# Moving small constant loads, value weights, the seam into attention, the gates and the operand sums of keys and values in a two-batch decoder kernel

## The chip, the core and the metric

The kernel is one program on one core of one Trainium2 chip. Its time is what the device needs for one execution, in microseconds (us). The engines of a core run side by side and wait for one another through semaphores: TensorE (PE in the profile) for matmuls, VectorE (DVE), ScalarE (ACT) and GpSimd (POOL) for elementwise work, and SyncE (SP), which here only issues transfers. All arithmetic is in float32 but for the quantized product, whose operands are whole numbers in bfloat16.

## The reference

Two batches of 512 tokens with 1024 features each, and a context of 1024 tokens for each batch, go through four residual steps. `ln` is a layer norm without weights.

```python
x = x + fake_quant(ln(x)) @ fake_quant(ctx)              # 8-bit grid, one scale and zero point a side
h = ln(x)                                                # 8 low-rank experts of rank 16, mixed
q = h[:, 179:-1, :].mean(1)                              # by a softmax over the mean token
r = softmax(q @ router_W.T + router_b)
x = x + h @ W.T + b + 2 * sum_e(r_e * (h @ A_e.T) @ B_e.T)
h = ln(x)                                                # 32 query heads, 8 key and value heads
Q, K = rope(h @ wq), rope(ctx @ wk); V = ctx @ wv
x = x + softmax(Q @ K.T / sqrt(128) + mask) @ V @ wo
h = ln(x)                                                # 4 experts of rank 8, the best one a token
x = x + h @ W_up.T + (h @ A_e.T) @ B_e.T, e = argmax(h @ gate_w.T + bias)
```

## The kernel before

**Products by seven.** Every large product is cut into two by two blocks and made with seven block products instead of eight, from sums of blocks. `left_steps` makes four sums for one side (`s1`, `s2`, a new `a21`, `s4`), `right_steps` four for the other (`t1`, `t2`, a new `b12`, `t4`), one instruction each. `seven` runs the block products in the order 1, 2, 6, 7, 5, 4, 3. Products 1 and 2 use blocks as they were loaded; product 6 wants `s2` and `t2`, product 7 the new `a21` and `b12`, product 3 `s4`, product 4 `t4`. Products 1 and 2 share one bank of PSUM (the accumulators beside TensorE), 7 and 4 another, 5 and 3 a third; VectorE reads a bank before the next product adds to it (L288 to L300). A block product of keys, queries or values is 4 or 8 matmuls and takes TensorE 3.43 us; a float32 matmul leaves two records in the profile.

**Stages.** In order: keys and values of batch 0 (`keys`, `values`, heads in two halves `q`), with the quantized product of batch 0 and then of batch 1 laced in (`layer_0` through `weave`); keys and values of batch 1, then with the layer norm and router of batch 0 (`routed`) laced in; the second step's products (`linear`); queries of both batches (`queries`), the last of them inside the beginning of attention; attention over 64 heads of queries with the output projection laced in; the last linear step, whose gates (`gated`) are laced into the end of attention.

**What sets the order.** TensorE's order is that of the program text throughout (`manual_schedule`). In the first product stage VectorE and ScalarE are written out by hand as well, and in attention VectorE, ScalarE and GpSimd. Elsewhere a planner orders each engine's queue, by the order of the text and by when it thinks that data and buffers are there. Each queue, SP's transfers included, runs strictly in the order that it was given. Buffers come from pools by size: 14 of 8 KB a partition (`u8`), 17 of 4 KB (`u4`), 10 of 2 KB (`u2`).

**The places of the change.** Eight small constants (four quantization parameters, two biases, the router's matrix `r0_t`, the gates' matrix `ga_t`) are loaded through POOL's queue at the start (L119 to L146). The first blocks of key weights and context are loaded in four chunks over SP's and ScalarE's queues, and `seven` starts with head group 0 (`m` is the head group in a pair). Value weights are loaded by `quad_weights` (L370) after the key products that stand before them, and summed by VectorE (L245 to L253). `routed` adds the bias on GpSimd (L612) and makes the router's logits with eight matmuls of 8 columns (L630). `queries` rotates heads (L216 to L223) on VectorE, for the last quarter of heads on GpSimd and one step later. In `attention` each head goes through three phases: scores with the mask added (L768, L782); the maximum's tree (L790 to L796) with projections or remaining query products between; then the maximum placed in PSUM (L810), subtracted (L814), the exponential (L817), its sums on GpSimd (L820 to L825) and the product with the values (L831). Maximum and denominator are turned by transposes (L732), written to DRAM as a row and read back to all partitions (L741, L747). At the start of attention `mid` is a head without an `old` one in front of it. `hooks` hangs the work of the last step on heads and phases; `gated` has five stretches: clear, two of matmuls, transposes with the choice of the expert, and the last transposes.

Of the kernel before, what the change touches and what calls it, by code (L numbers as in the profile page):

```python
# [12 lines left out]
F32 = mybir.dt.float32  # L13
BF16 = mybir.dt.bfloat16
AF = mybir.ActivationFunctionType
ALU = mybir.AluOpType
# [23 lines left out]
def decoder_kernel(  # L40
# [66 lines left out]
    make_identity(nc, ident)  # L107
    eps_t = const.tile([P, 1], F32, name="eps_t")
    nc.gpsimd.memset(eps_t, EPS)
    prefer = const.tile([P, E1], F32, name="prefer")  # L110
    for e in range(E1):
# [4 lines left out]
    qp = {}  # L116
    for name, ap in qparams.items():
        t = const.tile([P, 1], F32, name=f"qp_{name}")
        nc.gpsimd.dma_start(t, ap.partition_broadcast(P))  # L119
        qp[name] = t  # L120
    for side in ("x1", "x2"):
        t = const.tile([P, 1], F32, name=f"qp_inv_{side}")
        nc.vector.reciprocal(t, qp[f"{side}_scale"])
        qp[f"{side}_inv"] = t

    c_x1 = const.tile([P, 1], F32, name="c_x1")
    c_x2 = const.tile([P, 1], F32, name="c_x2")
    for c_t, side in ((c_x1, "x1"), (c_x2, "x2")):
        nc.vector.tensor_scalar(c_t, qp[f"{side}_zp"], -1.0, QMID, ALU.mult, ALU.add)
    kc2 = const.tile([P, 1], F32, name="kc2")  # L130
    nc.vector.tensor_scalar_mul(kc2, c_x2, float(D))
    s12 = const.tile([P, 1], F32, name="s12")
    nc.vector.tensor_tensor(s12, qp["x1_scale"], qp["x2_scale"], ALU.mult)
    ident_b = const.tile([P, P], BF16, name="ident_b")
# [3 lines left out]
    rb_t = const.tile([P, E0], F32, name="rb_t")  # L138
    nc.gpsimd.dma_start(rb_t, rb0.partition_broadcast(P))
    eb_t = const.tile([P, E1], F32, name="eb_t")  # L140
    nc.gpsimd.dma_start(eb_t, ebias.partition_broadcast(P))
    r0_t = const.tile([P, NC, E0], F32, name="r0_t")
    nc.gpsimd.dma_start(r0_t, r0T.rearrange("(c p) e -> p c e", p=P))
    NGA = E1 + E1 * R1
    ga_t = const.tile([P, NC, NGA], F32, name="ga_t")
    nc.gpsimd.dma_start(ga_t, gaT.rearrange("(c p) e -> p c e", p=P))  # L146
    cos_t = [const.tile([P, HALF], F32, name="cos_t"), None]
# [121 lines left out]

    def seven(product, emit):  # L270

        banks = {}
        for i in (1, 2, 6, 7, 5, 4, 3):
            first = {2: 1, 4: 7, 3: 5}.get(i, i)
            if i == first:
                banks[i] = ps_b()
            acc = banks[first]  # L280
            product(i, acc, i == first)
            if i == 1:
                u, c22, c21 = u2([P, HALF]), None, None
                nc.scalar.copy(u, acc)
            elif i == 2:
                emit(0, 0, acc)
            elif i == 6:
                nc.vector.tensor_tensor(u, u, acc, ALU.add)  # L288
            elif i == 7:
                c22 = u2([P, HALF])  # L290
                nc.vector.tensor_tensor(c22, u, acc, ALU.add)
            elif i == 5:
                nc.vector.tensor_tensor(c22, c22, acc, ALU.add)  # L293
                emit(1, 1, c22)
            elif i == 4:
                c21 = u2([P, HALF])
                nc.vector.tensor_tensor(c21, u, acc, ALU.add)
                emit(1, 0, c21)
            else:
                nc.vector.tensor_tensor(u, u, acc, ALU.add)  # L300
                emit(0, 1, u)
            yield
# [60 lines left out]

    def quad_weights(dram, q):

        raw = []
        for mh in range(2):
            for ch in range(2):
                w = u4([P, 4, 256])
                nc.sync.dma_start(w, dram[q, mh, ch])  # L370
                raw.append(w)
        return quad_sums(raw)

    def quad_sums(raw):
        return left_sums(nc.vector, *raw, lambda: u4([P, 4, 256]))

# [36 lines left out]
    def context_sums(quarters):  # L413
        return right_sums(nc.vector, *quarters, lambda: u8([P, 4, HALF]))

# [65 lines left out]

    def keys(b, q, ctx_ops, w):
        def group(m):
# [11 lines left out]

            return seven(product, emit)

# [111 lines left out]
    def routed(b, quarters, a_t, b_t, result):  # L609
# [14 lines left out]
        nc.vector.tensor_tensor(qm[:, 0, :], qm[:, 0, :], qm[:, 1, :], ALU.add)  # L624
        nc.vector.tensor_scalar_mul(qm[:, 0, :], qm[:, 0, :], 1.0 / (Q_END - Q_START))
        yield
        yield
        racc = ps_b()
        for c in range(NC):
            nc.tensor.matmul(  # L630
                racc[:, :E0],
                qm[:, 0, c : c + 1].to_broadcast([P, P]),
                r0_t[:, c, :],
                start=(c == 0),
                stop=(c == NC - 1),
            )
        lg = small([P, E0])
# [29 lines left out]

    def queries(q, h_ops, w, later=None):

        def head(m):  # L670
# [7 lines left out]
            def finish(i, j, src):  # L678
                dst = u2([P, HALF]) if (i, j) == (0, 0) else src
                eng = nc.vector if later is None else nc.gpsimd  # L680
                yield from rope_steps(dst, src, 0, ATT_SCALE, eng)
                nc.sync.dma_start(q_d[j][4 * q + 2 * i + m], dst)
# [173 lines left out]
    def attention(extra):  # L856
# [28 lines left out]
        for n in range(-2, total + GRP + 1):  # L885
# [33 lines left out]
            if n > GRP and gg + 1 < B * NKV:  # L919
                for i in {2: (1, 6, 2), 3: (7, 5, 4, 3)}.get(k, ()):  # L920
                    w_ops[i] = output_operand((gg + 1) % NKV, i)
            for _ in range(extra.pop(n, 0)):
                for _ in range(2):
                    next(tree, None)
                next(extra["products"])
            if n == GRP:
                w_ops = {i: output_operand(0, i) for i in (1, 6, 2, 7, 5, 4, 3)}
# [3 lines left out]

            if mid:
                mid.place_maximum()
# [5 lines left out]
            if old:  # L939
                old.attend(0)  # L940
            if mid:
                mid.exponential(0)
            if old:
                old.den = from_row(old.den)
                if new:
                    new.turn_maximum()
            if mid:
                mid.exponential(1)
            if new:
# [92 lines left out]

    for c in range(4):
        cs = slice(c, c + 1)
        nc.sync.dma_start(wk_raw[0][0][:, cs, :], wk[0, 0, 0][:, cs, :])
        load_context(nc.scalar, 0, 0, cs)
# [14 lines left out]
    for ch in range(2):  # L1061
        load_weight(1, 1, ch)


    ctx_ops = [ctx_raw[0], ctx_raw[2]] + [None] * 5
    w = [wk_raw[q][0:2] + [None] * 5 for q in range(2)]
    first = [keys(0, q, ctx_ops, w[q]) for q in range(2)]

# [7 lines left out]
    with tc.manual_schedule(engines={mybir.EngineType.DVE, mybir.EngineType.Activation}):  # L1076
        rights = right_steps(nc.vector, *ctx_raw, lambda: u8([P, 4, HALF]))
        lefts = left_steps(nc.vector, *wk_raw[0], lambda: u4([P, 4, 256]))
        advance(rights, 2)
        advance(lefts, 2)  # L1080
        for g in first[0]:
            next(g)
# [15 lines left out]
        load_rows(0, nc.scalar)  # L1098

    side = layer_0()  # L1100
    for b in range(B):
        if b == 1:
            for ch in range(2):
                ctx_raw[2 * ch + 1] = context_quarter(1, ch, 1, nc.scalar)
            w = quad_weights(wk, 0)
            ctx_ops = context_sums(ctx_raw)
        for i, stage in enumerate((keys, keys, values, values)):
# [6 lines left out]
            if (b, i) == (0, 1):  # L1114
                main = chain(*first[1])
            else:
                main = pair(*stage(b, i % 2, ctx_ops, w))
            weave(main, side, 2)
            if i < 3:
                w = quad_weights((wk, wv)[(i + 1) // 2], (i + 1) % 2)  # L1120
            if i == 1 and b == 1:
# [42 lines left out]
    h_ops = [hb[0][0], hb[0][1]] + [None] * 5  # L1164
    early = [head for q in range(2) for head in queries(q, h_ops, w[q])]
    for _ in range(2):
# [8 lines left out]
    for q in range(NH // 4):  # L1175
        heads = (
            early[2 * q : 2 * q + 2]
            if q < 2
            else queries(q, h_ops, w, later if q == NH // 4 - 1 else None)
        )  # L1180
        main = chain(*heads) if q < 2 else pair(*heads)
        for g in ((0,), (1,), (2,), (3,), (4,), (5,), (6, 7), ())[q]:
            output_sums(g)
        if q < NH // 4 - 1:
            for _ in main:
                pass
            if q > 0:
                w = quad_weights(wq, q + 1)

    extra = {-2: 3, -1: 3, 0: 2, 1: 2, 2: 2, 3: 1, 4: 1}
    steps = attention({**extra, "products": main, "later": later})
# [39 lines left out]
    for i in range(2):  # L1233
# [10 lines left out]
    ]  # L1244
    hooks[(62, 1)] = [lambda: advance(last["gates"], 3)]
    hooks[(62, 2)] = [
        lambda: fetch_weight(7, 0, 1),
        lambda: fetch_weight(3, 1, 1),
    ]
    with tc.manual_schedule(  # L1250
# [6 lines left out]
        for i in range(3 * (B * NH + 2)):  # L1257
# [4 lines left out]
            if (n - 2, phase) == (63, 1):  # L1262
                zT = next(last["gates"])
                h_ops, parts = last["h"], last["w"]
# [4 lines left out]
                main = linear(0, h_ops, w_ops, None, None)  # L1269
                advance(main, 2)  # L1270

    h_ops[:] = token_sums(last["hs"], lambda: u4([P, 4, 256]))
# [122 lines left out]
```

## Time and profile before

| | us |
|---|---|
| median of 3 runs | 2451.58 (2450.20 to 2452.53) |
| the profiled execution | 2450.07 |
| its span in the profile | 2448.30 |
| TensorE busy | 2412.5 (99%) |
| VectorE busy | 1841.1 (75%) |
| GpSimd busy | 1031.3 (42%) |
| ScalarE busy | 530.8 (22%) |

The profile is one execution, seen by the hardware profiler; a line names the engine, the line of the kernel (L355), the operation, the tile written and those read. A wait is put down to what ended last before it. Idle time of an engine counts only where it makes TensorE wait. Before 480 us GpSimd does eight additions in all, beside the issue of transfers and the setting of constants.

### The profile page before, as it was taken

What the parts mean: (1) busy time and instruction counts of PE and PEld (TensorE: products, weight loads), DVE (VectorE), ACT (ScalarE), POOL (GpSimd) and SP (SyncE); (2) the same over time, 40 slices, a digit from 0 to 9 for tenths busy, and PEclk for the clock granted to TensorE, in tenths of its full rate; (3) what the DMA queues carried; (4) which work ended last, traced back from release to release, by engine and by line L of the source; (5) the groups of instructions that cost most, each with busy time, mean ns of one, the idle gap of its engine ahead of it and who ended that gap; (6) DMA issues with size and microseconds to landing.
All of it is one profiled execution on the core that took longest, in us unless ns stands there. A gap on an engine that the chain in (4) does not pass through costs nothing.

```text
span 2448.3 us, 19583 instructions
## 1 busy us (share of the span) xinstructions
PE 2412.5 (99%) x6792; PEld 1195.8 (49%) x6800; DVE 1841.1 (75%) x1994; ACT 530.8 (22%) x623; POOL 1031.3 (42%) x550
## 2 busy tenths in 40 slices
PE   8999999999999999999999999999999999999999
PEld 3477458654444443444444444444444444444444
DVE  4949774345876556898888888888898998888653
ACT  1210221011222222322222222222222222222210
POOL 0000010210000001677676767667776767677621
PEclk9999999999999999999999999999999999999999
DMA  5537133013796221244323323442433343233501
GB/s 182 181 105 273 69 134 108 26 60 116 274 330 216 78 91 56 77 156 111 81 83 107 114 65 90 142 145 79 125 116 79 94 125 112 66 90 108 172 9 60
DMA packets 149010, 288.01 MB, mean 118 GB/s; under 512 B 29424, under 2 KB 47360, under 8 KB 146608
## 3 DMA queue, kind: packets, MB, share of 16 engines
q1 hardware_dynamic: 108080, 244.35, 29.9%
q10 hardware_dynamic: 40400, 41.70, 6.9%
q8 instruction: 54, 0.88, 0.2%
q0 software_dynamic: 432, 0.71, 0.1%
q14 instruction: 44, 0.36, 0.1%
HBM read 223.54 MB, written 63.18 MB: 117 GB/s over the span
## 4 chain that ended last, share of the span: by engine, by line
PE 60%; DVE 6%; POOL 2%; issue 1%; DMA 1%; ACT 1%; ACTq 0%; SPq 0%; DVEq 0%; POOLq 0%
PE b L355 26%; PE wide L768 16%; PE b L831 15%; PE wide L732 2%; DVE u L814 2%; DMA u<-in_wo_dram 1%; DVE u L782 1%; POOL u L823 0%; POOL u L824 0%; DVE small L734 0%; DVE u L792 0%; DVE u L794 0%; ACT u L817 0%; POOL u L825 0%; DVE u L328 0%
## 5 line engine op out<-in xcount | busy, mean ns | idle before, releaser
L355 PE MATMUL b<-u,u 128*128 128x512 f32 (+1 forms) x3616 | 1394.2, 542 | 21.3 <-DMA u<-in_ctxT_in_dram 7.6
L355 PEld LDWEIGHTS b<-u,u 128*128 128x128 f32 x3616 | 684.6, 191 | 695.9 <-issue 612.8
L768 PE MATMUL wide<-u,u 128*128 128x512 f32 x1024 | 454.8, 595 | 7.3 <-DVE u L782 6.4
L831 PE MATMUL b<-u,u 128*128 128x512 f32 x1024 | 460.3, 592 | 0.0
L782 DVE TENSOR_TENSOR u<-wide,u 128x1024 f32<-128x1024 f32 x256 | 312.8, 1224 | 130.3 <-PE wide L768 129.9
L817 ACT ACTIVATE u<-u 128x2048 f32<-128x2048 f32 x128 | 244.7, 1912 | 655.8 <-DVE u L814 593.9
L768 PEld LDWEIGHTS wide<-u,u 128*128 128x128 f32 x1024 | 193.4, 190 | 257.3 <-issue 177.9
L814 DVE TENSOR_TENSOR u<-u,b 128x2048 f32<-128x2048 f32 x128 | 290.2, 2268 | 0.0
L820 POOL TENSOR_TENSOR u<-u 128x1024 f32<-128x1024 f32 x64 | 151.5, 2367 | 317.5 <-ACT u L817 310.1
L831 PEld LDWEIGHTS b<-u,u 128*128 128x128 f32 x1024 | 186.2, 192 | 184.6 <-issue 184.6
L310 POOL TENSOR_TENSOR u<-u,u 128x512 f32<-128x512 f32 x120 | 188.5, 1597 | 175.4 <-DVE u L322 153.2
L328 DVE TENSOR_TENSOR u<-u,b 128x512 f32<-128x512 f32 x200 | 135.8, 680 | 126.0 <-PE b L355 125.9
L222 POOL TENSOR_TENSOR u<-u,sin_t 128x512 f32<-128x512 f32 x8 | 11.6, 1456 | 402.7 <-ACT u L217 402.7
L823 POOL TENSOR_TENSOR u<-u,u 128x1024 f32<-128x1024 f32 x64 | 150.7, 2354 | 36.4 <-ACT u L817 36.0
L824 POOL TENSOR_TENSOR u<-u,u 128x1024 f32<-128x1024 f32 x64 | 150.8, 2356 | 5.0
L842 POOL TENSOR_TENSOR u<-u,u 128x512 f32<-128x512 f32 x64 | 119.9, 1873 | 10.0 <-DMA u<-row 10.0
L216 ACT ACTIVATE u<-u 64x512 f32<-64x512 f32 x72 | 45.2, 628 | 356.3 <-DVE u L293 177.6
L790 DVE TENSOR_TENSOR u<-u 128x1024 f32<-128x1024 f32 x64 | 115.8, 1810 | 0.0
L732 PEld LDWEIGHTS wide<-ident,u 128*128 128x128 f32 x512 | 79.6, 203 | 63.9 <-issue 55.0
L612 POOL TENSOR_TENSOR u<-u,u 128x1024 f32<-128x1024 f32 x8 | 20.2, 2529 | 214.9 <-DVE u L168 111.6
L792 DVE TENSOR_TENSOR u<-u,u 128x1024 f32<-128x1024 f32 x64 | 105.4, 1646 | 0.2
L825 POOL TENSOR_TENSOR u<-u 128x512 f32<-128x512 f32 x64 | 101.0, 1578 | 5.0
(135 smaller groups left out, 1614.3 us busy)
## 6 DMA issues: line engine op xcount, KB each, us to landing
u<-row ACTq DMA_DIRECT2D x128, 256.0 KB, 3.7
u<-wo SPq DMA_DIRECT2D x64, 512.0 KB, 4.0
u<-in_wo_dram SPq DMA_DIRECT2D x48, 512.0 KB, 4.5
u<-in_wq_dram SPq DMA_DIRECT2D x32, 512.0 KB, 4.2
q<-u SPq DMA_DIRECT2D x64, 256.0 KB, 2.4
u<-in_wo_dram SPq DMA_DIRECT2D x16, 1024.0 KB, 8.2
wo<-u SPq DMA_DIRECT2D x32, 512.0 KB, 4.2
u<-q SPq DMA_DIRECT2D x64, 256.0 KB, 4.2
```

The lines of the kernel that those rows point to most:

```text
L310: nc.gpsimd.tensor_tensor(c, c, what, ALU.add)
L328: nc.vector.tensor_tensor(c, c, acc, ALU.add)
L355: nc.tensor.matmul(acc, lhsT, rhs, start=start and k == 0, stop=k == len(pairs) - 1, skip_group_check=True,)
L732: nc.tensor.transpose(tr[:, t, :], src[:, t, :], ident)
L768: nc.tensor.matmul(sc[:, ts(n, HALF)], self.kT[:, ts(2 * j + n, P)], self.qT, start=True, stop=True,)
L782: nc.vector.tensor_tensor(self.e[j // 2][:, js, :], sc.rearrange("p (k q) -> p k q", k=2), mask[j], ALU.add)
L814: nc.vector.tensor_tensor(e, e, self.nmf.unsqueeze(1).to_broadcast([P, 4, S]), ALU.add)
L817: nc.scalar.activation(e, e, AF.Exp)
L820: nc.gpsimd.tensor_tensor(d, e[:, 0:2, :], e[:, 2:4, :], ALU.add)
L823: nc.gpsimd.tensor_tensor(d, d, e[:, 0:2, :], ALU.add)
L824: nc.gpsimd.tensor_tensor(d, d, e[:, 2:4, :], ALU.add)
L831: nc.tensor.matmul(self.acc, self.v[:, k, :], self.e[j][:, k % 4, :], start=(k == 0), stop=(k == NKT - 1),)
```

## The change

It makes six edits. (1) The eight constant loads go from POOL's queue to SP's, behind the loads of the first stage; the first blocks come in three chunks instead of four, the last of double size; both head groups multiply each chunk as it lands (`begun`); and 20 matmuls of `ones_b` by itself are put in front of them, into a bank that the first product overwrites. (2) The raw value weights of batch 0 are taken and loaded before the key products of the second half instead of after them. (3) GpSimd makes the operand sums of keys and values: the six sets of weight sums behind the first two, and the context's sums of batch 1. (4) The router multiplies and adds over its eight chunks on VectorE, so that one matmul by ones is left of eight. (5) At the seam between queries and attention, the last rotation of the last quarter but one waits for attention's third phase; one query product moves from the first head to the second, and that head's exponentials go between the query products. In all heads the denominator's row is read after the second exponential. (6) The gates' transposes and choice come after the third phase of head 62, and their last transposes after two products of the last step.

```diff
-    for name, ap in qparams.items():
-        t = const.tile([P, 1], F32, name=f"qp_{name}")
-        nc.gpsimd.dma_start(t, ap.partition_broadcast(P))
...
-    nc.gpsimd.dma_start(r0_t, r0T.rearrange("(c p) e -> p c e", p=P))
...
-    def seven(product, emit):
+    def seven(product, emit, begun=None):
...
-                banks[i] = ps_b()
+                banks[i] = begun if begun is not None and i == 1 else ps_b()
             acc = banks[first]
-            product(i, acc, i == first)
+            if begun is None or i > 1:
+                product(i, acc, i == first)
...
-    def quad_weights(dram, q):
+    def quad_weights(dram, q, eng=nc.vector):
+        return quad_sums(raw_weights(dram, q), eng)
...
-        return right_sums(nc.vector, *quarters, lambda: u8([P, 4, HALF]))
+        return right_sums(nc.gpsimd, *quarters, lambda: u8([P, 4, HALF]))
...
+        nc.vector.tensor_tensor(
+            weighted,
+            r0_t.rearrange("p c e -> p e c"),
+            qm[:, 0, :].unsqueeze(1).to_broadcast([P, E0, NC]),
+            ALU.mult,
+        )
+        nc.vector.tensor_reduce(each, weighted, AX.X, ALU.add)
         yield
         yield
         racc = ps_b()
-        for c in range(NC):
-            nc.tensor.matmul(
-                racc[:, :E0],
-                qm[:, 0, c : c + 1].to_broadcast([P, P]),
-                r0_t[:, c, :],
...
+        nc.tensor.matmul(
+            racc[:, :E0], one_t.to_broadcast([P, P]), each, start=True, stop=True
+        )
...
-            for _ in range(extra.pop(n, 0)):
+            for i in range(extra.pop(n, 0)):
                 for _ in range(2):
                     next(tree, None)
                 next(extra["products"])
+                if mid and not old and i == 1:
+                    mid.place_maximum()
+                    mid.exponential(0)
+                if mid and not old and i == 2:
+                    mid.exponential(1)
...
-            if mid:
+            if mid and old:
                 mid.place_maximum()
...
             if old:
                 old.attend(0)
-            if mid:
-                mid.exponential(0)
-            if old:
-                old.den = from_row(old.den)
+                if mid:
+                    mid.exponential(0)
                 if new:
                     new.turn_maximum()
-            if mid:
-                mid.exponential(1)
+                if mid:
+                    mid.exponential(1)
+                old.den = from_row(old.den)
...
-    for c in range(4):
-        cs = slice(c, c + 1)
+    for c in range(3):
+        cs = slice(c, c + 1 + c // 2)
         nc.sync.dma_start(wk_raw[0][0][:, cs, :], wk[0, 0, 0][:, cs, :])
         load_context(nc.scalar, 0, 0, cs)
...
+    for name, ap in qparams.items():
+        nc.sync.dma_start(qp[name], ap.partition_broadcast(P))
+    nc.sync.dma_start(rb_t, rb0.partition_broadcast(P))
+    nc.sync.dma_start(eb_t, ebias.partition_broadcast(P))
+    nc.sync.dma_start(r0_t, r0T.rearrange("(c p) e -> p c e", p=P))
+    nc.sync.dma_start(ga_t, gaT.rearrange("(c p) e -> p c e", p=P))
...
+    begun = [ps_b() for _ in range(2)]
+    for i in range(20):
+        nc.tensor.matmul(begun[0][:, :P], ones_b, ones_b, start=True, stop=True)
+    first = [keys(0, 0, ctx_ops, w[0], begun), keys(0, 1, ctx_ops, w[1])]
...
+        for c in range(4):
+            for m in range(2):
+                nc.tensor.matmul(
+                    begun[m],
+                    wk_raw[0][0][:, c, ts(m, P)],
+                    ctx_raw[0][:, c, :],
...
-            w = quad_weights(wk, 0)
+            w = quad_weights(wk, 0, nc.gpsimd)
...
                 main = chain(*first[1])
+                raw = raw_weights(wv, 0)
+                weave(main, side, 2)
+                w = quad_sums(raw, nc.gpsimd)
             else:
                 main = pair(*stage(b, i % 2, ctx_ops, w))
-            weave(main, side, 2)
-            if i < 3:
-                w = quad_weights((wk, wv)[(i + 1) // 2], (i + 1) % 2)
+                weave(main, side, 2)
+                if i < 3:
+                    w = quad_weights((wk, wv)[(i + 1) // 2], (i + 1) % 2, nc.gpsimd)
...
+            last_two = q >= NH // 4 - 2
+            heads = queries(
+                q, h_ops, w, (nc.vector, nc.gpsimd)[q == NH // 4 - 1], later if last_two else None
+            )
...
+            for i, _ in enumerate(main):
+                if i < 13:
+                    for rotation in later:
+                        next(rotation, None)
+                    later.clear()
...
-    extra = {-2: 3, -1: 3, 0: 2, 1: 2, 2: 2, 3: 1, 4: 1}
+    extra = {-2: 2, -1: 4, 0: 2, 1: 2, 2: 2, 3: 1, 4: 1}
...
-    hooks[(62, 1)] = [lambda: advance(last["gates"], 3)]
+    hooks[(62, 1)] = [lambda: advance(last["gates"], 2)]
     hooks[(62, 2)] = [
+        lambda: next(last["gates"]),
...
-                zT = next(last["gates"])
...
                 advance(main, 2)
+                zT = next(last["gates"])
```

## The prediction

> **What bounds the kernel now.** I read the page first, then TensorE's waits, the busy time by windows, and the instructions in order of time around every gap. TensorE is the bound:
>
> ```profile
> span 2448.3 us, 19583 instructions
> ...
> PE 2412.5 (99%) x6792; PEld 1195.8 (49%) x6800; DVE 1841.1 (75%) x1994; ACT 530.8 (22%) x623; POOL 1031.3 (42%) x550
> ```
>
> The change can only earn TensorE's 36 idle us, its time at half clock, and the few matmuls it removes. The waits name the places:
>
> ```profile
> PE b L355 <- DMA u<-in_ctxT_in_dram: 7.6, 4, 3.9
> PE wide L768 <- DVE u L782: 6.4, 6, 3.6
> PE b L355 <- DMA u<-in_wv_dram: 4.1, 1, 4.1
> PE b L355 <- DVE u L291: 2.9, 3, 1.8
> PE b L355 <- ACT u L320: 2.5, 1, 2.5
> ```
>
> Columns: total, times, longest. In order: first loads, seam into attention, value weights, a late eviction, end of attention. Idle time costs twice. Of the windows I asked for, two stretches of 3.41 us have TensorE fully busy and the granted clock (the seventh figure, after POOL's) at 0.50, just behind the gaps at 110.16 and 970.59:
>
> ```profile
> 114.56:117.97 3.41, 3.41 (x9) 2.70 (x8) 3.41 (x8) 1.55 (x3) 0.00 (x0) 0.50 0.99 320
> 974.72:978.13 3.41, 3.41 (x5) 1.33 (x4) 1.16 (x2) 0.23 (x1) 3.25 (x3) 0.50 0.13 45
> ```
>
> Each adds 3.41/2 = 1.71 us. The first 19 us are slow too, though those windows print a clock of 1.00: weight loads start 0.86 us apart up to 18.17 and 0.43 apart from 19.01.
>
> **The change part by part.** Sums stand against the profiled execution, 2450.07 us (span plus 1.77); the median of the runs, 2451.58, lies 1.5 above it.
>
> *Start.* Matmuls begin at 3.88 and are fed by chunks landing at 3.84, 6.02, 10.33 and 13.70 (context, ScalarE's queue). Head group 0 runs first, group 1 after the fourth chunk. From 13.74 ten matmul records remain of these eight products: six at 0.86 until 18.99, four at 0.43, so they end at 20.7. Now both groups use each chunk as it lands, and chunks three and four come as one transfer, which is issued with the first three (the third was issued at 1.67, the fourth only at 3.86). The eight small POOL transfers, whose packets hold the DMA engines between 8 and 14 us, go behind the large loads. The merged chunk lands between 9.5 (just under the third now) and 13.7 (the fourth now); I take 11, since the bytes ahead are the same and only the POOL packets are gone. Four matmuls remain: 3.4 us at full clock, 6.9 at half, so 14.4 to 17.9. The next product needs the other half of the context, which landed at 17.36 and lands perhaps 1.5 sooner: 15.8 to 16.2 binds. 20.7 - 16.2 = 4.5 us; range 2.5 to 6.5. The 20 added matmuls run before 3.88: eight bf16 ones of this shape take 0.61 us at full clock, so 20 take 3.1 at half, beginning at 1.0 when `ones_b` is set (ends 4.1; worst price 0.2). The moved constants cost SP eight issues of 0.3 to 0.9 us after 21.5, before it first waits for a key store at 35.5: nothing. If that cover went, it would cost a key store's delay, which nobody awaits. The six small VectorE instructions on them (0.15 each) and the added memset (0.10) find those engines idle.
>
> The Trainium skill (TensorE: Matmul & The Clock Gate, Part 1) says that the clock opens after a free-running window of about 3.4 us of activity; by its 107 ns a cold matmul, an estimate, the warm-up lasts 2.1 us and fills no window alone. By the page the clock would then open one window into the chunk matmuls, and the sum would keep 4.5, for loads bind either way.
>
> *Value weights.* The load sits on SP behind key stores that wait for VectorE:
>
> ```profile
> 92.08 18.25 SPq L494 DMA_DIRECT2D kT<-u  x4
> 110.38 0.42 SPq L370 DMA_DIRECT2D u<-in_wv_dram  x1
> ```
>
> It is issued 0.2 us after TensorE runs dry and lands at 114.22. Taken before the weave, the loads have two spare `u4` buffers and those that `a11` and `a12` free by 42, a lap of 60 us ahead. The loads of quantization rows queue behind them for buffers, but four buffers come free between 62 and 73. Gain 4.10 + 1.71 = 5.8; I take 5.3, lower end 1.7 (the clock window only).
>
> *Router.* Sixteen records hold TensorE for 1.70 us, twice (the second at about 505):
>
> ```profile
> 406.50 1.85 PE L630 MATMUL b<-r_t,small 128*128 128x8 f32 x16
> ```
>
> One matmul, two records, takes some 0.3: 2 x 1.4 = 2.8 us. The added product and reduction on VectorE (64 elements; 0.2 us each by L638 and L624) precede two yields, that is several products, and hide there.
>
> *Seam.* Gaps of 1.40 at 933.64 and 3.60 at 970.59: scores wait for buffers that L782 empties, and L782 stands behind the last query rotation (three of 0.69) and behind two L814 (4.47). The deferred rotation runs after the first scores; the exponentials run between four query products of 3.43, while no scores wait. Gaps and clock window come to 6.7. Behind L814 now wait L288 and L291, which free TensorE's buffers; the maximum's row (3.7 us to land) must be there a product sooner; and the first transposes run a product earlier, at some 945.5 instead of 948.9, with the maximum's tree done at 944.4, so 1.1 is left. I take 5.3, range 2 to 6.7. In steady state only the issue of the denominator's load moves past an activation of 1.9 us; the normalisation it feeds comes 11 us after that issue at 2247.54: nothing.
>
> *Gates.* TensorE waits 0.48 for L975 and 2.48 for L320, which stands on ScalarE behind an exponential held by the 3.9 us gate chain on VectorE (2280.1 to 2284.1). The chain moves behind both L814, its last transpose behind two products. What is late next is L322 behind the chain. Gain 2.3 of 3.0; range 0.5 to 3.0.
>
> *GpSimd.* Six sets of weight sums (four adds of 128x1024) and one of context sums (four of 128x2048) leave VectorE. The price is in these lines:
>
> ```profile
> 326.50 1.22 DVE L250 TENSOR_TENSOR u<-u,u 128x1024 f32<-128x1024 f32 x1
> 332.65 2.83 DVE L222 TENSOR_TENSOR u<-u,sin_t 128x512 f32<-128x512 f32 x1
> 332.12 2.81 POOL L612 TENSOR_TENSOR u<-u,u 128x1024 f32<-128x1024 f32 x1 [100.78 <-PE b L355]
> ```
>
> An add of this size takes 1.22 on VectorE and 2.35 alone on GpSimd (L823). And L222, otherwise 0.68, ended only when the GpSimd add was over: VectorE instructions with two SBUF operands wait for it. L168 (one operand) is stretched too, from 0.81 to 1.83 at most; those that read PSUM are not (L291 0.68). GpSimd gets 24 x 2.35 + 4 x 4.70 = 75.2 us, VectorE loses 24 x 1.23 + 4 x 2.29 = 38.7. Four L612 adds (10.8 us) in a dense stretch of VectorE held L291 and gave TensorE's 1.81 us at 342: 0.17 us of wait per GpSimd us; four others in loose stretches gave none. Dense here are the first value set (VectorE is busy 45.2 of the 50.2 us ahead of it), the second batch's key and context set (56.6 of 60 at 196 to 256), and its value set at 323: 9.4 + 28.2 + 9.4 = 47 us, x 0.17 = 8 us lost. Ends: 2 gained (the 342 wait goes), and 36.5 lost (75.2 - 38.7 all on the path). Nearest are the L612 rows, so 8. TensorE can also wait for the sums themselves: the second batch's key weights landed at 227.6, and if GpSimd makes the four weight sums first, the second context sum is done 4 x 2.35 + 2 x 4.70 = 18.8 later, at 246.4; the third product wants it after four of 3.43 and two turns of a row, from 233.9 on, at 248. That margin of 1.6 may go either way and stays in the ends.
>
> The Trainium skill (GPSIMD Engine Reference, Engine selection) speaks against this move: elementwise work with two inputs belongs on VectorE, GpSimd being about 2x slower. By that rule the sums would stay, and the sum below would be 20.2 instead of 12.2.
>
> Sum: 4.5 + 5.3 + 2.8 + 5.3 + 2.3 = 20.2 gained, 8 lost, net 12.2: 2437.9, or 2439 with the runs' offset.
>
> **The rivals.** *GpSimd holds VectorE, slower.* Evictions queue in order behind blocked rotations and quantization, and a lag over one product (3.43 us) stops TensorE; counting eight products back from 110.16, the L291 at 85.11 starts 2.4 after its product and ends 0.3 in time. For: VectorE is idle under 0.6 us from 77 to 120 and from 207 to 256. Against: TensorE waits for only three L291 now. It is slower by 4.9 us from 25.1 us of loss, 0.33 per GpSimd us everywhere, twice the dense rate; with all 36.5 it gives 2450.1 - 20.2 + 36.5 = 2466, typically 2460. *The waits only move.* First loads stay bound by bandwidth, value loads by buffers, the seam waits for the row: lower ends 2.5 + 1.7 + 2.5 + 2 + 0.5 = 9.2, less 8: 2449, 2450 with the offset. *GpSimd free.* VectorE's slack absorbs the blocks, and the evictions stay in time: 20.2 to 24.8 gained (the upper ends), 2430 to 2425, 2427 to 2431 with the offset.
>
> **How the numbers follow.** Chances: forecast 0.55, GpSimd free 0.17, moved waits 0.15, slower 0.13. The limit of 0.2% (about what a measurement can tell from no change) is 4.9 us. Faster: 0.50 + 0.17 + 0.03 = 0.70; same: 0.05 + 0.11 = 0.16; slower: 0.13 and a remainder, 0.14. The range runs from GpSimd free to past the moved waits, 2427 to 2455; the forecast's own is 2432 to 2446.
>
> **What would show it.** Right: the eighth product done by 16 us; no wait for in_wv_dram and none of 3.6 at L768; L630's matmuls down from 32 records to 4; one clock window at 0.50 fewer at 114 and at 974; L222, L223 and L197 up to 2.8 us long where GpSimd adds. Wrong: TensorE waiting for L291 or L293 by over 10 us in all, or for GpSimd's sums.

## The result and the profile after

The changed kernel takes 2472.84 us (median of 5 runs, 2469.78 to 2473.93) against 2451.58 before: a ratio of 1.0084 (95% interval 1.0070 to 1.0098). It is 21 us slower, where 12.6 us faster was forecast, and beyond the range. The profiled execution took 2473.93 us with a span of 2472.0. Line numbers have moved up: product matmuls are L345 (before L355), evictions L278, L281, L283, L287 and L290 (L288, L291, L293, L297, L300), the quantization L182, L185, L186 (L194, L197, L198), its scaling L156 (L168), rotations L207, L210, L211 (L219, L222, L223), weight sums L233 to L241, context sums L247 to L255.

The first lines of the page of the changed kernel:

```profile
span 2472.0 us, 19556 instructions
...
PE 2413.3 (98%) x6792; PEld 1196.7 (48%) x6792; DVE 1853.4 (75%) x1970; ACT 527.5 (21%) x623; POOL 1108.5 (45%) x571
```

TensorE has the work of before (2413.3 us busy, 2412.5 before) and stands 23 us longer. VectorE, which by the prediction's sum had 38.7 us less to do, is busy 12 us longer. TensorE's waits name the place (total, times, longest):

```profile
PE b L345 <- DVE u L281: 37.9, 5, 20.9
PE b L345 <- DVE u L283: 5.6, 4, 3.3
PE wide L763 <- DVE u L777: 2.2, 5, 0.6
PE b L345 <- DVE u L287: 2.0, 1, 2.0
...
PE b L1095 <- DMA u<-in_ctxT_in_dram: 0.6, 1, 0.6
```

The first loads (7.6 before), the value weights (4.1) and the seam's scores (6.4) are gone or small. The wait for the late eviction, 2.9 before, is now 37.9, and 31.6 of it are two stalls: 10.72 us at 100 and 20.88 at 229. Half clock goes with them; in these answers for windows the seventh figure is the granted clock:

```profile
104.94:115.18 10.24, 4.50 (x6) 1.92 (x7) 10.24 (x19) 0.01 (x1) 0.00 (x0) 0.50 0.14 51
231.24:255.13 23.89, 5.18 (x12) 4.19 (x13) 19.31 (x9) 0.00 (x0) 17.43 (x6) 0.50 0.07 27
```

TensorE works 4.50 and 5.18 us in them at half clock, which costs half of that, 2.3 and 2.6. Behind the next two stalls (2.03 at 365 and 5.19 at 372) stretches of 3.41 and 6.83 us follow, with TensorE busy for 3.41 and 4.09; half clock costs some 8.6 us in all.

Why L281 is late is seen where GpSimd and VectorE stand side by side in time. First GpSimd's context sums and first weight sums, then VectorE from the same moment on (a count behind x joins neighbours of one kind into one line):

```profile
217.98 5.05 POOL L247 TENSOR_TENSOR u<-u,u 128x2048 f32<-128x2048 f32 x1 [21.23 <-DVE u L186]
223.11 4.84 POOL L250 TENSOR_TENSOR u<-u,u 128x2048 f32<-128x2048 f32 x1
227.92 4.94 POOL L252 TENSOR_TENSOR u<-u,u 128x2048 f32<-128x2048 f32 x1
232.83 4.94 POOL L255 TENSOR_TENSOR u<-u,u 128x2048 f32<-128x2048 f32 x1
237.73 2.78 POOL L233 TENSOR_TENSOR u<-u,u 128x1024 f32<-128x1024 f32 x1
```

```profile
217.87 5.72 DVE L182 TENSOR_SCALAR u<-u,qp_x_inv,qp_x_zp 128x1024 f32<-128x1024 f32 x2
223.51 0.67 DVE L290 TENSOR_TENSOR u<-u,b 128x512 f32<-128x512 f32 x1
224.11 9.31 DVE L185 TENSOR_SCALAR u<-u 128x1024 f32<-128x1024 f32 x2
233.34 7.72 DVE L186 TENSOR_SCALAR u<-u 128x1024 bf16<-128x1024 f32 x2
240.98 2.82 DVE L156 TENSOR_SCALAR u<-u,small,small 128x1024 f32<-128x1024 f32 x1
243.73 0.68 DVE L278 TENSOR_TENSOR u<-u,b 128x512 f32<-128x512 f32 x1
244.32 2.23 DVE L182 TENSOR_SCALAR u<-u,qp_x_inv,qp_x_zp 128x1024 f32<-128x1024 f32 x1
246.59 2.71 DVE L185 TENSOR_SCALAR u<-u 128x1024 f32<-128x1024 f32 x1
249.22 0.67 DVE L281 TENSOR_TENSOR u<-u,b 128x512 f32<-128x512 f32 x1
```

L185 and L186 take 0.68 us each where GpSimd does nothing. Here two L185 take 9.31 together and two L186 7.72: a held instruction ends some 0.55 us after a GpSimd addition ends (the second L185 at 233.42, L252 at 232.86; the second L186 at 241.06, L233 at 240.51). The evictions L290, L278 and L281 read PSUM and keep their 0.67, but L281 stands in order behind seven held instructions and L278, which fill 25.1 us (224.11 to 249.22) instead of some 5.7 (five of 0.68, two of 0.81, one of 0.68). That difference, 19.4 us, is nearly the whole stall of 20.88. At 96 to 104 the same is seen with rotations: three take 2.82 or 2.83 us instead of 0.68 beside additions of 128x1024; the first is

```profile
96.05 2.83 DVE L210 TENSOR_TENSOR u<-u,sin_t 128x512 f32<-128x512 f32 x1
```

The stalls at 365 and 372 lie beside additions that the change did not move, GpSimd's four bias additions (L605, before L612):

```profile
356.65 2.79 POOL L241 TENSOR_TENSOR u<-u,u 128x1024 f32<-128x1024 f32 x1
359.40 5.54 POOL L605 TENSOR_TENSOR u<-u,u 128x1024 f32<-128x1024 f32 x2
```

In the kernel before they were spread from 332.12 to 348.09 and TensorE lost 1.81 us. Now they stand on GpSimd's queue behind the four value sums and come close together, from 359.40 to 371.66; with the half clock that follows TensorE loses 11 us.

A second wait is new: 3.3 us at 82.7 for L283. It stands on VectorE behind the quantization (L182) of a context row that landed late:

```profile
84.50 0.81 DVE L182 TENSOR_SCALAR u<-u,qp_x_inv,qp_x_zp 128x1024 f32<-128x1024 f32 x1 [1.75 <-DMA u<-in_ctx_in_dram]
85.23 0.68 DVE L283 TENSOR_TENSOR u<-u,b 128x512 f32<-128x512 f32 x1
```

SyncE's queue shows why (issue, length, transfer):

```profile
57.17 0.83 SPq L363 DMA_DIRECT2D u<-in_wv_dram  x1
66.27 0.32 SPq L487 DMA_DIRECT2D kT<-u  x1
66.64 0.92 SPq L363 DMA_DIRECT2D u<-in_wv_dram  x2
71.41 0.33 SPq L487 DMA_DIRECT2D kT<-u  x1
71.83 0.38 SPq L363 DMA_DIRECT2D u<-in_wv_dram  x1
72.30 0.40 SPq L414 DMA_DIRECT2D u<-in_ctx_in_dram  x1
75.36 0.33 SPq L487 DMA_DIRECT2D kT<-u  x1
75.78 6.55 SPq L414 DMA_DIRECT2D u<-in_ctx_in_dram  x6
```

The four value weights took the first places that came free; the rows (L414, before L421) begin at 72.3, and six are issued close together. Before, the first was issued at 64.2, although the start then took 7 us longer.

What went well is seen too. At the start the warm-up and the first sixteen matmul records run through:

```profile
1.06 2.31 PE L1078 MATMUL b<-ones_b 128*128 128x128 bf16 x20 [1.06 <-DVE ones_b L129]
3.94 9.81 PE L1095 MATMUL b<-u,u 128*128 128x512 f32 x16 [0.57 <-DMA u<-in_ctxT_in_dram]
```

The eighth matmul of these products ends at 13.7 (20.7 before), and the clock is full from 9.37 (18.99 before). The router's matmuls are 4 records of about 0.2 us instead of 32, the gates' gaps are gone, and the seam keeps small ones:

```profile
963.41 7.11 PE L763 MATMUL wide<-u,u 128*128 128x512 f32 x16 [0.45 <-DMA u<-q]
...
981.70 3.70 PE L763 MATMUL wide<-u,u 128*128 128x512 f32 x8 [0.41 <-DVE u L777]
...
996.95 3.27 PE L345 MATMUL b<-u,u 128*128 128x512 f32 x7 [1.25 <-DVE u L278]
```

### The profile page after: what moved, and what is told of

Read it like the earlier page. It is cut to its first block, busy times and chain, and to the rows that moved or that the text cites. A ratio compares the mean times of both kernels' runs of the same rounds, so it can differ in the third digit from the quotient of the medians.

```text
span 2472.0 us, 19556 instructions
## 1 busy us (share of the span) xinstructions
PE 2413.3 (98%) x6792; PEld 1196.7 (48%) x6792; DVE 1853.4 (75%) x1970; ACT 527.5 (21%) x623; POOL 1108.5 (45%) x571
## 4 chain that ended last, share of the span: by engine, by line
PE 53%; DVE 5%; issue 1%; POOL 0%; ACT 0%; POOLq 0%; ACTq 0%; DVEq 0%
PE b L345 19%; PE wide L763 16%; PE b L826 16%; PE wide L727 2%; DVE u L809 1%; DVE u L789 0%; DVE u L787 0%; DVE u L318 0%; DVE small L729 0%; DVE u L777 0%; PE b L967 0%; PE wide L192 0%; DVE u L791 0%; DVE small L151 0%; POOL u L818 0%
## 5 line engine op out<-in xcount | busy, mean ns | idle before, releaser
L345 PE MATMUL b<-u,u 128*128 128x512 f32 (+1 forms) x3600 | 1389.6, 543 | 48.2 <-DVE u L281 37.9
L345 PEld LDWEIGHTS b<-u,u 128*128 128x128 f32 x3600 | 682.7, 191 | 720.9 <-issue 605.1
L300 POOL TENSOR_TENSOR u<-u,u 128x512 f32<-128x512 f32 x120 | 184.4, 1562 | 170.7 <-DVE u L312 151.7
L233 POOL TENSOR_TENSOR u<-u,u 128x1024 f32<-128x1024 f32 x6 | 15.3, 2554 | 268.8 <-DMA u<-in_wv_dram 111.9
L837 POOL TENSOR_TENSOR u<-u,u 128x512 f32<-128x512 f32 x64 | 115.4, 1804 | 18.0 <-DMA u<-row 17.9
L787 DVE TENSOR_TENSOR u<-u,u 128x1024 f32<-128x1024 f32 x64 | 107.3, 1677 | 0.2
L789 DVE TENSOR_TENSOR u<-u,u 128x1024 f32<-128x1024 f32 x64 | 95.5, 1492 | 0.1
```

The costliest lines, as they stand in the source:

```text
L300: nc.gpsimd.tensor_tensor(c, c, what, ALU.add)
L345: nc.tensor.matmul(acc, lhsT, rhs, start=start and k == 0, stop=k == len(pairs) - 1, skip_group_check=True,)
```

## The experiments

Theory A: GpSimd's long additions hold VectorE's instructions until they end, and evictions wait behind these in order. Theory B: the loss comes from the new order of loads. Each kernel was timed beside the kernel before, which took 2451.27, 2452.06 and 2451.31 us (medians) on the three occasions; ratios are to that, with a 95% interval.

**The sums back on VectorE, and the sums alone on GpSimd.** The first is the changed kernel with one edit undone, the second the kernel before with that edit alone.

```diff
-        return right_sums(nc.gpsimd, *quarters, lambda: u8([P, 4, HALF]))
+        return right_sums(nc.vector, *quarters, lambda: u8([P, 4, HALF]))
...
-                w = quad_sums(raw, nc.gpsimd)
+                w = quad_sums(raw, nc.vector)
...
```

> The changed kernel with all operand sums of keys and values back on VectorE; the other five edits stay. Theory A (VectorE instructions with two SBUF operands, or with one in the fast mode, stand still while GpSimd adds, and the evictions queued behind them hold TensorE): the waits for L281 of 10.7 and 20.9 us and the 5.2 us one at 372 go, with the half clock behind them, 45 to 50 us in all: 2423 to 2430. Theory B (the early value loads take buffers and queue places, so that VectorE waits in order for quantization rows): the waits at 83 and 100 us stay, and so does the one at 229, which has no GpSimd part in it: 2465 to 2473.

> The kernel before with only the operand sums of keys and values moved to GpSimd. Theory A: it loses what the changed kernel loses there, 35 to 45 us net of the late eviction that the kernel before already had: 2485 to 2497, with TensorE waiting for L291 by over 25 us. Theory B: no early value loads, so within 5 us of the kernel before. The prediction's price was 8 us: 2460.

Measured: 2440.71 us, 0.9954 (0.9941 to 0.9966), for the first; 2480.64, 1.0118 (1.0102 to 1.0133), for the second. So the sums on GpSimd cost 2472.84 - 2440.71 = 32.1 us in the changed kernel and 2480.64 - 2451.27 = 29.4 on the kernel before. Theory A holds for the main loss, though the second kernel is 4 us faster than its range. The waits of that kernel, with the old order of loads, show it by itself:

```profile
PE b L355 <- DVE u L291: 25.8, 4, 19.1
```

But the first kernel is 10 us slower than A expected. Its waits show what is left:

```profile
PE b L345 <- DVE u L283: 5.8, 4, 3.3
PE b L345 <- DVE u L281: 4.5, 5, 1.6
PE b L345 <- ACT u L274: 4.4, 2, 4.1
```

The 3.3 us behind the late row is there with all sums on VectorE: a part of theory B.

**The same additions in shorter pieces.** In the changed kernel each operand sum on GpSimd is made by four instructions, or by eight (the code shows four, and one of the sums).

```diff
+    def add_in_parts(eng, out, x, y, op):
+        if eng is nc.gpsimd and len(out.shape) == 3 and out.shape[1] == 4:
+            for k in range(4):
+                eng.tensor_tensor(out[:, k, :], x[:, k, :], y[:, k, :], op)
+        else:
+            eng.tensor_tensor(out, x, y, op)
...
-        eng.tensor_tensor(s1, a21, a22, ALU.add)
+        add_in_parts(eng, s1, a21, a22, ALU.add)
...
```

> The changed kernel with each of GpSimd's sums of keys and values cut into four instructions of a quarter's length; the same arithmetic. By the rows of before (1.27 us for 512 columns, 2.35 for 1024) GpSimd's total rises from 75 to about 90 us. Theory A with the hold lasting one instruction: VectorE gets in four times as often and waits a quarter as long, so the waits for L281 fall from 38 us to about 10: 2435 to 2448. If VectorE is held in proportion to GpSimd's total time, whatever the length of one: 2473 to 2485. Theory B: 2471 to 2476.

> The changed kernel with each of GpSimd's operand sums cut into eight instructions. In one piece the sums cost 32.1 us against the same sums on VectorE (2472.8 against 2440.7), in four 5.9 (2446.6). Theory (VectorE is held until GpSimd's instruction ends, so the length of one decides): 2440 to 2446, less than in four pieces. Rival (GpSimd's total time decides, and eighths add start-up to it): 2447 to 2452.

Measured: 2446.62 us, 0.9981 (0.9971 to 0.9990), and 2445.03, 0.9977 (0.9967 to 0.9987). GpSimd's time on the sums goes up, from 83 us to 115 and 132, and the price against the sums on VectorE falls from 32.1 to 5.9 and 4.3. So it is the length of one instruction that holds, not the total. In the kernel with quarters, at the place of the great stall, VectorE has

```profile
219.89 2.84 DVE L185 TENSOR_SCALAR u<-u 128x1024 f32<-128x1024 f32 x2
222.66 3.43 DVE L186 TENSOR_SCALAR u<-u 128x1024 bf16<-128x1024 f32 x2
```

that is 1.4 and 1.7 us each instead of 4.7 and 3.9. Eight pieces bring nothing measurable beyond four. In that kernel a sum itself comes too late once, with half clock behind it; of its waits:

```profile
PE b L354 <- POOL u L235: 5.2, 1, 5.2
```

**The context sums alone back on VectorE.**

```diff
-        return right_sums(nc.gpsimd, *quarters, lambda: u8([P, 4, HALF]))
+        return right_sums(nc.vector, *quarters, lambda: u8([P, 4, HALF]))
```

> The changed kernel with only the context's four sums of 128x2048 back on VectorE; the weights' sums stay on GpSimd. Theory A: of the 20.9 us wait at 229 and its half clock some 16 go, since four holds of 4.9 us go and four of 2.7 stay; the waits at 100 and 372 stay: 2453 to 2460. Theory B: no difference over 3 us.

Measured: 2457.71 us, 1.0025 (1.0015 to 1.0035). The four additions of 128x2048, 19.8 us of GpSimd, cost 15.1 us, 0.76 for each us; the 24 of 128x1024, 63.5 us of GpSimd, cost the other 17.0, 0.27 for each. Some 9 of these 17 lie at the bias additions that stand behind the sums: this kernel has the two stalls too (2.12 and 5.20 us), and the one with all sums on VectorE has 1.60 there.

**One input instead of two on GpSimd.**

```diff
+    def add_in_parts(eng, out, x, y, op):
+        if eng is nc.gpsimd and len(out.shape) == 3 and out.shape[1] == 4:
+            eng.tensor_scalar(out, x, 1.0, None, ALU.mult)
+        else:
+            eng.tensor_tensor(out, x, y, op)
...
```

> The changed kernel with each of GpSimd's operand additions replaced by one multiplication of its first operand by 1 (one input instead of two, same sizes, same order and waits; the sums are not made). Theory (an instruction of two inputs on GpSimd is what holds VectorE): VectorE's 128x512 and 128x1024 instructions keep their 0.68 and 0.7 to 0.8 us beside it, 2430 to 2442. Rival (any long GpSimd instruction on SBUF holds VectorE until its end): the waits behind held VectorE instructions stay in proportion to their length, 2455 to 2473.

Measured: 2456.09 us, 1.0022 (1.0012 to 1.0032), at the lower end of the rival's range. The VectorE lines of this kernel show a mixture. Beside multiplications of 128x1024 (2.97 us in the mean), at 96 to 106, five instructions take 1.2 to 1.5 us and others between them keep their 0.68; beside those of 128x2048 (5.83 us each), L185 and L186 are held in full:

```profile
96.02 1.52 DVE L210 TENSOR_TENSOR u<-u,sin_t 128x512 f32<-128x512 f32 x1
...
99.27 1.52 DVE L182 TENSOR_SCALAR u<-u,qp_x_inv,qp_x_zp 128x1024 f32<-128x1024 f32 x1
...
217.53 11.02 DVE L185 TENSOR_SCALAR u<-u 128x1024 f32<-128x1024 f32 x2
228.47 11.60 DVE L186 TENSOR_SCALAR u<-u 128x1024 bf16<-128x1024 f32 x2
```

So two inputs on GpSimd are not needed for the full hold. What makes the shorter ones milder was not settled.

**No sums at all.**

> The changed kernel without the operand sums that it gave to GpSimd, on any engine (products take raw blocks in their place): what the move could bring at most. Theory (VectorE's relief is worth only the short waits that its own sums leave; the rows' late loads at 83 us stay): 2431 to 2438, that is 3 to 10 us below the 2440.7 with the sums on VectorE. Rival (VectorE was the hidden limit and its 38.7 us come back in good part): below 2428.

Measured: 2432.68 us, 0.9928 (0.9913 to 0.9943). To free VectorE of these sums can bring some 2440.71 - 2432.68 = 8.0 us in this kernel: that was the prize against which 32.1 were paid.

**The value weights: late as before, and behind the rows.** Both have the sums on VectorE. The first loads the value weights where the kernel before does; the second puts their loads behind the four pairs of rows:

```diff
                 main = chain(*first[1])
-                raw = raw_weights(wv, 0)
-                weave(main, side, 2)
+                for k, _ in enumerate(main):
+                    if k % 2 == 0:
+                        next(side, None)
+                    if k == 6:
+                        raw = raw_weights(wv, 0)
```

> The changed kernel with all operand sums back on VectorE and the value weights loaded and summed behind the key products as in the kernel before. Theory (the early loads cost more than they bring): the gaps at 83, 102, 107 and 122 us of the kernel with early loads (9.2 us and 3.4 for two half-clock stretches) go, the old ones near 110 and 127 (5.7 and 1.7) come back: 2451.3 less start 7.1, router 2.8, seam 6.4 and gates 3.0 is 2432, and 2430 to 2436. Rival (the early loads are worth their 5.3 us as predicted, and the missing 10 us lie elsewhere): 2444 to 2448.

> The changed kernel with all operand sums back on VectorE, and the raw value weights loaded inside the weave, behind the four pairs of context rows of the quantized product instead of ahead of them. That kernel without this second edit took 2440.7. Theory (early value loads took the queue places of the rows: four loads between 57 and 72 us, the rows only from 72.6 on, VectorE held in order for a row that landed at 84.9): the gap of 3.3 us at 83 goes with its half-clock stretch of 3.41 (1.7 us), and VectorE's work spreads again: 2431 to 2436. Rival (VectorE is simply too full between 81 and 122 us, whatever the order of the loads): within 2.5 us of 2440.7, other gaps of the same sum in place of the 3.3.

Measured: 2431.30 us, 0.9918 (0.9904 to 0.9931), and 2432.19, 0.9921 (0.9908 to 0.9935). The early loads as the change makes them thus lose 9.4 us (2440.71 - 2431.30; either interval is 3 us wide to each side, and in the two profiles stalls and half clock up to 130 us differ by some 6). Behind the rows they lose nothing and bring nothing. The rows are issued from 57.02 on instead of 72.57, the stall at 83 is gone, the value weights have landed by 93.3, and TensorE waits at 114 for something else (lines of TensorE, then of ScalarE):

```profile
119.68 9.76 PE L345 MATMUL b<-u,u 128*128 128x256 f32 x32 [5.67 <-ACT u L274]
```

```profile
118.56 0.29 ACT L163 ACTIVATE small<-small,eps_one 128x1 f32<-128x1 f32 x1 [0.85 <-DVE small L152]
...
119.04 0.59 ACT L274 COPY u<-b 128x512 f32<-128x512 f32 x1 [0.19 <-ACT small L163]
```

L274 copies the first value product out of its bank, into which the second product adds. It stands behind a layer norm's square root (L163), which waits for VectorE's statistics (L152), which stand behind the four value sums. With 6.83 us of half clock this costs what the load in time had gained.

**The start alone, and router, seam and gates alone,** on the kernel before.

> The kernel before with the start alone changed: constants behind the first loads, three chunks, both head groups on each chunk, 20 warm-up matmuls. By the forecast it gains 4.5 (2.5 to 6.5): 2446.8. By the trace of the changed kernel, where the eighth product ended at 13.6 instead of 20.7, it gains 7.1: 2444.2 (2443 to 2445.5). Rival (the later waits at 110 and 127 us take the lead up again): within 2 us of 2451.3.

> The kernel before with router, seam and gates alone changed (the last three edits). By the forecast 2.8 + 5.3 + 2.3 = 10.4 gained: 2440.9. By the gaps that are missing in the trace of the changed kernel, 2.8 + 6.4 + 3.0 = 12.2: 2439.1 (2438 to 2441). Rival (the row of the first maximum becomes the late one, or the denominator's later load costs in 64 heads): 2445 to 2452.

Measured: 2444.45 us, 0.9972 (0.9963 to 0.9982), 7.6 gained; and 2435.91, 0.9937 (0.9923 to 0.9950), 16.1 gained, more than either reading of it. In that profile TensorE's wait for the value weights ends 1.7 us sooner (108.29 + 4.25 against 110.16 + 4.10), ahead of all three edits: half clock ends at 15.92 there, at 18.99 before. Of the 16.1, with 10.4 for the three edits by their gaps, 4 us are left; the interval is 3 wide to either side. Some 2.4 of them lie in the middle of attention: from the 17th to the 121st subtraction of the maximum (L814) the kernel before takes 1088.4 us, this one 1086.1. Ten of the eleven kernels with these edits take 1085.1 to 1086.8 there (the one without sums 1088.4), the two others without them 1089.5 and 1089.9. In these heads the edits change only the place where the denominator's row is read, which the prediction had put at nothing; it was not run by itself.

**A version that beats both.** From the version with value loads behind the rows: the four value sums go behind the stage's first products, so that VectorE reaches the statistics sooner; and each of the four bias additions on GpSimd (L605, before L612) is cut into four.

```diff
-                w = quad_sums(raw, nc.vector)
+                w = raw[0:2] + [None] * 5
...
+                    for k, _ in enumerate(main):
+                        if k % 2 == 0:
+                            next(side, None)
+                        if k == 1:
+                            w[:] = quad_sums(raw, nc.vector)
...
-            nc.gpsimd.tensor_tensor(rows(b, t), rows(b, t), b_t, ALU.add)
+            for k in range(4):
+                c = ts(k, D // 4)
+                nc.gpsimd.tensor_tensor(rows(b, t)[:, c], rows(b, t)[:, c], b_t[:, c], ALU.add)
```

> The version with all sums on VectorE and the value weights loaded behind the rows (2432.2), with two more edits: the first value set's four sums are written behind the stage's first products instead of ahead of them, and the four bias additions on GpSimd are cut into four instructions each. In the former version TensorE stood 5.67 us at 114, since the first value product's copy on ScalarE stood behind square roots that waited for VectorE, full with the sums, and 6.83 us at half clock followed; and 1.59 us at 336 behind a rotation held by an addition on GpSimd. Theory (the sums' place and the length of GpSimd's instructions make these waits): 2.5 to 9 us less at 114 and 1 to 1.6 less at 336: 2422 to 2429. Rival (VectorE is full there with or without them, waits only move): 2430 to 2434.

Measured: 2424.16 us, 0.9894 (0.9877 to 0.9910), 27 us less than before. In its lines of TensorE the 5.67 at 114 is 1.10, and the 1.59 at 336 is 0.22:

```profile
111.54 3.72 PE L345 MATMUL b<-u,u 128*128 128x256 f32 x16 [1.10 <-ACT u L274]
```

```profile
330.66 14.69 PE L345 MATMUL b<-u,u 128*128 128x512 f32 x51 [0.22 <-DVE u L281]
```

From 10.2 to 2420.0 us of its span of 2420.9 the clock is full. The two edits were run together; the places tell them apart.

## Why the prediction was wrong

| term | forecast, us | measured, us | from |
|---|---|---|---|
| start | 4.5 gained (2.5 to 6.5) | 7.6 gained | the start alone |
| value weights | 5.3 gained (1.7 to 5.8) | 9.4 lost | with and without, sums on VectorE |
| router | 2.8 gained | 28 records fewer | rows |
| seam | 5.3 gained (2 to 6.7) | 4.6 gained | gaps and clock |
| gates | 2.3 gained (0.5 to 3.0) | 3.0 gained | gaps |
| GpSimd | 8 lost (2 gained to 36.5 lost) | 32.1 lost | sums back on VectorE |

The measured terms, with 2.8 for the router, come to 23.5 us lost; the kernel lost 21.3. The middle of attention gains some 1.9 besides (1088.4 to 1086.6 us).

*GpSimd: that it holds VectorE was seen; which instructions it holds and what that costs were wrong, by a factor of four.* The step that failed is the rate of 0.17 us of wait for each us of GpSimd, from four L612 additions in one dense stretch. It took the price as proportional to GpSimd's time, and the quarters show that it is not: more time, a fifth of the price. The very additions from which the rate was read cost TensorE 11 us, half clock included, instead of 1.81 when they came behind the sums. Two readings made the rate so small. First, the prediction held that VectorE instructions with two SBUF operands wait and that one with one operand is merely stretched, to 1.83 us at most. In the changed kernel that very instruction (L156) takes 2.82, and the quantization's one-operand instructions, which in the kernel before are some 25 of VectorE's 56.6 us at 196 to 256, are held to the end. Second, a row of held instructions ahead of an eviction adds up: seven of them made 25 us against the 3.4 us that a product lasts, while two held L222 (2.83 us at 332.65, 2.84 at 338.09) ahead of L291 made 1.8. The context additions had no row of their size in the trace of before; at 4.9 us each they hold for longer than a product lasts.

The Trainium skill (GPSIMD Engine Reference, Specifications) says that GpSimd shares its SBUF interfaces with VectorE and contends with instructions that have two SBUF inputs or run in a two-port performance mode. The rotations' 0.68 to 2.83 us and L185's 0.68 to 4.7 agree with this if L185 runs in such a mode, which no run here shows; the page gives no size. The multiplications of 128x2048 show that one input on GpSimd's side is enough.

*Value weights: the sign was wrong.* The step that failed is "four buffers come free between 62 and 73": the value weights, for which the prediction had buffers free by 42, were issued from 57.17 to 71.83 and took the places of the rows. The forecast looked at when the rows would find buffers, not at what stood behind them: the second row lands at 84.47 (70.65 with the value weights behind the rows) and holds VectorE in order, and an eviction with it. And the gain was counted to the full though the wait was only shown to end last there: with the weights in time, the copy L274 is late, by 4.1 us with the early loads and by 5.7 with the loads behind the rows.

*Start: the size was off, to the good side.* The last term of the sum, the other half of the context, was put at 15.8 to 16.2 us by 1.5 sooner than before; its two parts landed at 11.9 and 12.1 (17.4 and 16.6 before), and the merged chunk at 9.31 (11 taken). The clock opened 5.4 us into the chunk matmuls (3.94 to 9.37), where the prediction's estimate had one window of 3.4. What the 20 matmuls have in this was not run by itself.

*Router, seam and gates* went as forecast by their gaps, and gained more than that when run alone: the seam keeps 0.45 and 0.41 of 1.40 and 3.60, loses the clock window of 1.7, and pays 1.25 for L278, named as what is late next.

*The rival "GpSimd holds VectorE, slower"* was the right story, with 0.13. Its threshold of 25.1 us was passed by the sums alone. Its price of 2460 to 2466 was short by 7 us at its upper end: the value weights came out 14.7 us worse than forecast, the start 3.1 better, and GpSimd cost 32.1 of the 36.5. The sign named for it, TensorE waiting for L291 or L293 by over 10 us, is what the profile shows: 43.5 us (37.9 + 5.6). As a threshold 10 us was too low: 10.3 (4.5 + 5.8) are left with all sums on VectorE.

## What to carry to other kernels

Before giving GpSimd elementwise work, look at what VectorE does at that time: if its queue holds evictions that another engine waits for, the price here was up to the length of one GpSimd instruction for each held VectorE instruction in front of the eviction, so cut the work into short instructions or leave it. Look also at what stands behind the new work on GpSimd's queue: here the bias additions, delayed and pushed together, made some 9 of the 32 us. A load that is moved forward takes buffers and a queue's place from what came first: follow the displaced loads to the instruction that waits for them. What ends a wait last is not all that is late: count the gain only up to the next one.

## What was not expected of the hardware

GpSimd's additions of 128x2048 hold one-operand VectorE instructions with 128x1024 elements in float32, too: 0.68 us becomes 4.7, while an eviction that reads PSUM keeps its 0.67 in the same stretch. One-input multiplications on GpSimd were no shorter than additions (2.97 us for 128x1024, where additions took 2.3 to 3.3), held VectorE fully at 128x2048 and slowed only some of its instructions, to 1.2 to 1.5 us, at 128x1024. Small pieces have a price of their own: the sums took GpSimd 83 us in one piece each, 115 in four and 132 in eight.
